# A graph layer on one core: which units of the last stage are scaled ahead and transposed, which are multiplied

## The chip, the core and the metric

The kernel runs on one core of a Trainium2 chip. A core has TensorE (PE in the profile, with its weight loads as PEld), VectorE (DVE), ScalarE (ACT), GpSimd (POOL) and SyncE (SP, which here only issues DMAs), a working memory of 128 partitions (SBUF), and PSUM, into which TensorE writes its results. The metric is the device time of one execution in microseconds; a time without an addition is the median of several runs.

## The reference

A graph layer over 12500 nodes with 256 features, a mixture of experts, a batch norm over the nodes, and a layer norm around all of it. What matters here is the end:

```python
def _forward(feats, ...):
    ...                                   # graph convolution m @ W_gc, residual, experts
    y = x + core                          # core: top-2 mixture of 64 experts
    mean = jnp.mean(y, axis=0)            # over the 12500 nodes, per feature
    var = jnp.mean((y - mean) ** 2, axis=0)
    return (y - mean) * jax.lax.rsqrt(var + BN_EPS) * gamma + beta

def _layernorm(x, axis=-1, eps=1e-05):    # over the 256 features, per node
    m = jnp.mean(x, axis=axis, keepdims=True)
    v = jnp.var(x, axis=axis, keepdims=True)
    return (x - m) / jnp.sqrt(v + eps)

out = _layernorm(x + _forward(x, ...))
```

## The kernel before

The nodes lie in 98 tiles of 128 (the last has 84). The program runs the edges and the first half of the experts, then the second half of the experts, then the last stage, which begins at line 2804 and is the only one that the change touches.

Through the whole last stage `y` lies in `acc`, seen as `acc2`: features on the partitions, in two halves `h` of 128, nodes along the free dimension. The loop at line 2825 adds the last contributions (line 2839), turns them (lines 2850 and 2851), takes the batch statistics (line 2857) and copies the sums back into `acc2` (line 2859). Lines 2880 to 2904 then make from the statistics, on VectorE, the scale `amp` and the shift `base` of each feature, and two diagonal matrices, `d_amp` and `d_base`.

From line 2905 on the nodes go through in 14 units. `order` (line 2861) numbers them: unit 0 is tiles 0 to 7, units 1 and 2 are the single tiles 96 and 97, units 3 to 13 are the other tiles in eights. `sets` (line 2862) groups them: [0], [1, 2], [3, 4], [5, 6], [7, 8], [9, 10], [11, 12], [13]. The input rows of unit u are in `xt[u]`, called `z`, [128 nodes x 8 tiles x 256], loaded by `fetch` (line 2865): the first ten ahead, unit u + 10 once unit u is handed out.

TensorE brings two tiles at a time back to nodes on the partitions, into a PSUM tile `q`, of which the pool `ps2` has five. There are two forms:

- **Scaled ahead and transposed** (`by_act`, before: odd units). First `acc2` of the unit is scaled and shifted in place, one instruction per half of 1024 columns: on GpSimd for units 1, 3 and 5 (line 2927), on ScalarE for units 7, 9, 11 and 13 (line 2932). Then TensorE transposes each half of each tile (line 2949).
- **Product** (before: even units). TensorE multiplies ones by `d_base` (line 2941) and adds each half times `d_amp` (line 2951); nothing is done ahead.

VectorE adds `q` to `z` and takes the row statistics, in one of two ways:

- **Squared** (before: units 0, 4, 6, 8, 10): one instruction per tile (line 2954) adds and also writes the row sum into a column of `m`; ScalarE then takes the sum of squares per tile (line 2968).
- **Otherwise**: an addition for two tiles (line 2961) and `bn_stats` for each (line 2963); a chain of eight small operations makes `m` and `ve` of them (lines 2975 to 2982), on GpSimd, in the last two sets on VectorE (`V_`).

At the end of a set: square root on ScalarE (line 2986), five small operations (lines 2987 to 2992, on VectorE but for the first), then each tile is normalised in place with one instruction: on GpSimd (line 3003) for units of eight with an even number, on ScalarE (line 3008) for the others; unit 13 is divided among three engines. The unit is handed out by a DMA of 1 MB on SP (line 3016); units 11, 12 and 13 go in two halves.

The small tiles of a set (`st`, `m`, `gap`, `ve`, `less`, `rs`, `rsq`, lines 2906 to 2912) come from the pool `two` with two buffers each, so a set's first write into `m` has to wait until an earlier set has given its buffer back, and the last reader of `m` is the normalisation.

The order of the instructions on each engine is chosen by a planner before the run, by the order of the program and by its own estimate of when operands are ready; each engine then runs its queue strictly in that order. Inside `tc.manual_schedule(engines=...)` the engines named keep the program's order.

Of the kernel before, what the change touches and what calls it, by code (L numbers as in the profile page):

```python
# [8 lines left out]
F32 = mybir.dt.float32  # L9
# [4 lines left out]
AF = mybir.ActivationFunctionType  # L14
ALU = mybir.AluOpType
# [4 lines left out]
P = 128  # L20
N = 12500
D = 256
# [3 lines left out]
EPS = 1e-5  # L26
# [140 lines left out]
def gnn_moe_kernel(  # L167
# [37 lines left out]
    def rows(t):  # L205
        return P if t < NT - 1 else RAG
# [191 lines left out]
    a = 0  # L398
# [10 lines left out]
    a = 0  # L409
# [2394 lines left out]
    with ExitStack() as stack:  # L2804
# [100 lines left out]
        for g, units in enumerate(sets):  # L2905
# [3 lines left out]
            m, gap, ve, less, rs, q_ = (  # L2909
# [4 lines left out]
            V_ = GP if g < len(sets) - 2 else V  # L2914
            at = 0
            for u in units:
                t0, n = order[u]
                r = rows(t0)
                z = xt[u][:r, :n]

                by_act = u % 2

                squared = not by_act and n == 8 and u != 12
                for h in range(2 * by_act):
                    y = acc2[:, h, t0 * P : (t0 + n - 1) * P + r]
                    if u in (1, 3, 5):
                        GP.tensor_scalar(
                            y, y, amp[:, h : h + 1], base[:, h : h + 1],
                            op0=ALU.mult, op1=ALU.add,
                        )  # L2930
                        continue
                    S.activation(
                        y, y, AF.Identity, bias=base[:, h : h + 1], scale=amp[:, h : h + 1]
                    )
                for i in range(0, n, 2):
                    k = min(2, n - i)
                    q = ps2.tile([P, 4, P], F32, name="q")
                    for j in range(k):
                        t = t0 + i + j
                        if not by_act:  # L2940
                            T.matmul(
                                q[:r, 2 * j : 2 * j + 2].rearrange("p a b -> p (a b)"),
                                ones_f[:, :r], d_base.rearrange("p a b -> p (a b)"),
                                start=True, stop=False,
                            )
                        for h in range(2):
                            to, y = q[:r, 2 * j + h], acc2[:, h, t * P : t * P + r]
                            if by_act:
                                T.transpose(to, y, ident)
                            else:  # L2950
                                T.matmul(to, y, d_amp[:, h], start=False, stop=h == 1)
                    if squared:
                        for j in range(k):
                            V.scalar_tensor_tensor(
                                z[:, i + j], q[:, 2 * j : 2 * j + 2].rearrange("p a b -> p (a b)"),
                                1.0, z[:, i + j], op0=ALU.mult, op1=ALU.add,
                                accum_out=m[:, at + i + j : at + i + j + 1],
                            )
                        continue
                    zi = z[:, i : i + k].rearrange("p t d -> p (t d)")  # L2960
                    V.tensor_add(zi, q[:r, : 2 * k].rearrange("p a b -> p (a b)"), zi)
                    for j in range(k):
                        V.bn_stats(st[:r, at + i + j], z[:, i + j])
                of = slice(at, at + n)
                if squared:
                    V.tensor_scalar_mul(m[:, of], m[:, of], -1.0 / D)
                    for i in range(n):
                        S.activation(
                            two.tile([P, D], F32, name="junk"), z[:, i], AF.Square,
                            bias=m[:, at + i : at + i + 1],  # L2970
                            accum_out=ve[:, at + i : at + i + 1],
                        )
                    V_.tensor_scalar(ve[:, of], ve[:, of], 1.0 / D, EPS, op0=ALU.mult, op1=ALU.add)
                else:
                    V_.tensor_sub(gap[:, of], st[:, of, 1], st[:, of, 4])
                    V_.tensor_mul(gap[:, of], gap[:, of], gap[:, of])
                    V_.tensor_scalar(gap[:, of], gap[:, of], 0.25, EPS, op0=ALU.mult, op1=ALU.add)
                    V_.tensor_add(ve[:, of], st[:, of, 2], st[:, of, 5])
                    V_.tensor_scalar(ve[:, of], ve[:, of], 1.0 / D, None, op0=ALU.mult)
                    V_.tensor_add(ve[:, of], ve[:, of], gap[:, of])  # L2980
                    V_.tensor_add(m[:, of], st[:, of, 1], st[:, of, 4])
                    V_.tensor_scalar(m[:, of], m[:, of], -0.5, None, op0=ALU.mult)
                at += n
# [10 lines left out]
            for u in units:  # L2994
# [3 lines left out]
                for i in range(n):  # L2998
                    by = GP if u % 2 == 0 and n == 8 else S
# [17 lines left out]
                fetch(u + 10)  # L3017

# [40 lines left out]
```

## Time and profile before

| | us |
|---|---|
| median of 3 runs | 2768.57 |
| lowest and highest run | 2766.28, 2773.52 |
| the profiled execution | 2766.83 |
| its span, first to last instruction | 2765.0 |
| of it: edges and first half of the experts, about | 2196 |
| second half of the experts, about | 443 |
| last stage, from its first loads on, about | 126 |

Over the whole span TensorE is busy 2389.1 us, GpSimd 1991.3, VectorE 1736.7 and ScalarE 687.6. These sums say little about the last 126 us, in which the change lies. How to read what follows: a timeline row has the start, the duration from the first start to the last end, the engine, the line, the operation with output and inputs, how many instructions it merges, and in brackets the engine's idle time before it and who ended it. A window row has for one stretch the busy time of each engine with its count of instructions, TensorE's granted clock as a share of the full one, the mean share of time that the 16 DMA engines were busy, and GB/s.

### The profile page before, as it was taken

How to read it: one execution, taken by the hardware profiler on the slowest of the kernel's cores; microseconds unless marked ns; L12 is line 12 of the kernel's file. 1: busy time of each engine (PE TensorE's matmuls, PEld its weight loads, DVE VectorE, ACT ScalarE, POOL GpSimd, SP SyncE). 2: the span in 40 equal slices, each digit the busy share in tenths (PEclk: the TensorE clock that was granted, in tenths of full speed). 3: DMA queues.
4: the chain of work that ended last, by engine and by line, in shares of the span. 5: the costliest groups of instructions: out<-in, count | busy, mean ns of one | idle time of the engine just before them, and what ended most of it. 6: DMA issues, size and time to landing. Idle time of an engine off the chain costs nothing.

```text
span 2765.0 us, 44989 instructions
## 1 busy us (share of the span) xinstructions
PE 2389.1 (86%) x13077; PEld 1830.1 (66%) x13077; DVE 1736.7 (63%) x7803; ACT 687.6 (25%) x2124; POOL 1991.3 (72%) x2240
## 2 busy tenths in 40 slices
PE   3967777777888887777999999999999899999986
PEld 3745555554666654545777777877768588988865
DVE  8979998754778864554655444454445645555558
ACT  1824344431111101101111111111111222222236
POOL 8777777777777777777777777777777666767615
PEclk9978999998999999997999999999999999999998
DMA  6963333336655555555677767877778778999888
GB/s 216 332 197 104 106 106 111 106 111 220 199 156 158 161 157 163 157 148 170 186 233 210 216 207 230 250 233 238 240 243 262 228 243 248 289 296 309 282 282 268
DMA packets 328938, 571.85 MB, mean 207 GB/s; under 512 B 79126, under 2 KB 229286, under 8 KB 328678
## 3 DMA queue, kind: packets, MB, share of 16 engines
q1 hardware_dynamic: 218424, 291.06, 33.1%
q0 software_dynamic: 96432, 263.13, 32.1%
q10 hardware_dynamic: 13822, 14.65, 1.7%
q8 instruction: 107, 1.75, 0.3%
q14 instruction: 153, 1.25, 0.1%
HBM read 494.61 MB, written 73.97 MB: 206 GB/s over the span
## 4 chain that ended last, share of the span: by engine, by line
PE 43%; POOL 19%; DMA 14%; issue 12%; DVE 7%; ACT 0%; SPq 0%; POOLq 0%; DVEq 0%; ACTq 0%
POOL ring L984 18%; DMA ring<-h_d,src_col 12%; PE p L1001 9%; PE yp L2357 8%; PE hp L2330 6%; PE bank L1225 3%; PE bank L1788 2%; PE yp_a L1788 2%; PE yp_a L1754 2%; PE bank L1754 2%; PE bank L1230 1%; POOL acc L1677 1%; PE yp_a L1162 1%; DVE acc L268 1%; PE xtp L2312 1%
## 5 line engine op out<-in xcount | busy, mean ns | idle before, releaser
L984 POOL DMA_INDIRECT ring<-h_d,src_col x1489 | 1416.6, 951 | 467.5 <-issue 402.0
L1001 PE MATMUL p<-ring,o 128*128 128x257 f32 (+1 forms) x3042 | 958.4, 419 | 246.6 <-DMA ring<-h_d,src_col 220.9
L1001 PEld LDWEIGHTS p<-ring,o 128*128 128x128 f32 x3042 | 526.7, 199 | 441.9 <-DMA ring<-h_d,src_col 311.3
L973 DVE TENSOR_SCALAR_CACHE_REDUCE o<-lane,rel 128x128 f32<-128x128 f32 x1489 | 450.4, 337 | 107.9 <-PE p L1001 107.1
L2357 PE MATMUL yp<-w,h 128*128 128x256 f32 (+4 forms) x968 | 225.1, 379 | 0.0
L1970 ACT ACTIVATE acc<-lane_b,acc 125x128 bf16<-125x128 bf16 x544 | 167.5, 389 | 177.9 <-DVE acc L1092 75.1
L2330 PE MATMUL hp<-xT,w 128*128 128x112 f32 (+17 forms) x1040 | 193.2, 332 | 1.8 <-DVE xT L2314 1.8
L2357 PEld LDWEIGHTS yp<-w,h 128*128 128x128 f32 (+4 forms) x968 | 169.5, 180 | 30.9 <-issue 0.9
L268 DVE TENSOR_TENSOR acc<-tab,acc 125x2450 bf16<-125x2450 bf16 (+1 forms) x136 | 184.4, 1356 | 3.9 <-PE bank L1979 3.2
L2330 PEld LDWEIGHTS hp<-xT,w 128*128 128x128 f32 x1040 | 163.2, 193 | 18.9 <-issue 2.9
L2335 ACT ACTIVATE h<-hp,b 128x112 f32<-128x112 f32 (+15 forms) x260 | 94.8, 417 | 321.7 <-issue 174.2
L1765 ACT ACTIVATE acc<-yp_a,acc 128x112 f32<-128x112 f32 (+19 forms) x150 | 57.8, 432 | 403.5 <-PE yp_a L1754 356.4
L1788 PE MATMUL bank<-acc 128*128 128x256 f32 (+7 forms) x672 | 156.1, 383 | 0.0
L1788 PEld LDWEIGHTS bank<-acc 128*128 128x128 f32 (+7 forms) x672 | 117.9, 178 | 28.5 <-issue 4.0
L2290 POOL DMA_INDIRECT xg<-xb_d,tables x101 | 97.4, 964 | 50.2 <-PE yp L2357 10.7
L1677 POOL DMA_INDIRECT acc<-xa_d,tables x110 | 104.2, 947 | 33.5 <-issue 31.4
L1754 PE MATMUL yp_a<-acc 128*128 128x112 f32 (+20 forms) x600 | 122.9, 346 | 1.7 <-DMA acc<-in_wpack 1.6
L1225 PE MATMUL bank<-wcat,acc 128*128 128x320 f32 x388 | 123.2, 442 | 0.0
L2384 POOL DMA_INDIRECT z_d<-yo,tables x81 | 81.5, 1006 | 55.5 <-DVE yo L2383 34.4
L1975 PEld LDWEIGHTS <-acc 125*128 125x128 bf16 x1156 | 83.1, 100 | 57.2 <-DVE acc L1092 15.8
L973 DVE DVE_READ_ACCUMULATOR o<-lane,rel 128x1 f32 x1489 | 119.4, 80 | 0.0
L1765 ACT ACTIVATE acc<-bank,acc 128x144 f32<-128x144 f32 (+18 forms) x106 | 44.8, 455 | 294.5 <-PE bank L1754 250.1
(452 smaller groups left out, 3943.2 us busy)
## 6 DMA issues: line engine op xcount, KB each, us to landing
acc<-in_wpack SPq DMA_DIRECT2D x128, 512.0 KB
w<-in_wpack SPq DMA_DIRECT2D x128, 512.0 KB
ring<-h_d,src_col POOLq DMA_INDIRECT x1489
tables<-h_d SPq DMA_DIRECT2D x99, 128.0 KB
z<-in_x SPq DMA_DIRECT2D x12, 1024.0 KB
acc<-in_x SPq DMA_DIRECT2D x13, 896.0 KB
h_d<-acc SPq DMA_DIRECT2D x13, 896.0 KB
zt<-z_d SPq DMA_DIRECT2D x22, 512.0 KB
```

The lines of the kernel that those rows point to most:

```text
L268: V.tensor_tensor(o.rearrange("p k (a b) -> p k a b", b=2), lane_b[:p, None, :n] .rearrange("p k (a b) -> p k a b", b=2) .to_broadcast([p, ...
L973: o_last[u] = V.tensor_scalar(o_of[u][:, j], lane, rel[:, c : c + 1], None, op0=ALU.is_equal, op1=ALU.add, accum_out=o_sum[:, c % 16 : c % ...
L984: i = GP.indirect_dma_start(out=h_row[:, :D], out_offset=None, in_=x if c < NE else h_d, in_offset=bass.IndirectOffsetOnAxis(ap=src_col[:, ...
L1001: i = T.matmul(p_of[g][:, :n], o_of[v][:, m], h_row[:, :n], start=j == 0, stop=last)
L1225: chain["dense"] = T.matmul(g[:r], acc2[:, k, a : a + r], wcat[:, k], start=k == 0, stop=k == 1 and not early,)
L1677: GP.indirect_dma_start(out=g, out_offset=None, in_=xa_d, in_offset=bass.IndirectOffsetOnAxis(ap=dense_a[:, c : c + 1], axis=0),)
L1754: T.matmul(hp, w1[:, c, j * P : (j + 1) * P], xT[:, c, :m], start=c == 0, stop=c == 1,)
L1765: S.activation(h1[:, j, :m], hp_of.pop((q, j)), AF.Gelu, bias=b1_a[i % 2][:, j : j + 1])
L1788: T.matmul(y, h1[:, j, k * P : k * P + n], w2[:, j], start=j == 0, stop=j == 3)
L1970: S.activation(s_los[k % 3][:, j], lane_b[:EP], AF.Sign, bias=nbs[u % 2][:, i, j : j + 1])
L2330: T.matmul(v, w1[:, c, j * P : (j + 1) * P], xT[:, c, :m], start=c == 0, stop=c == 1,)
L2357: T.matmul(yp[:r], h1[:, j, a : a + r], w2[:, j], start=j == 0, stop=j == 3,)
```

## The change

Five edits, all in the loop over units:

1. The form of the units. Scaled ahead and transposed are now units 0, 1, 3, 4, 6, 8, 10, 12 (before 1, 3, 5, 7, 9, 11, 13); product are 2, 5, 7, 9, 11, 13.
2. Unit 0 goes in pieces of 1, 1, 2, 2 and 2 tiles. Each piece is scaled by itself, the first on VectorE, the others on ScalarE. For the others GpSimd scales 1, 3, 4, 6 and ScalarE 8, 10, 12.
3. Squared are now units 3, 5, 7, 9, 11, so the first unit of each pair instead of the second.
4. GpSimd normalises units 3, 5, 7, 9, 12 (before 0, 4, 6, 8, 10, 12), ScalarE the others; unit 13 as before.
5. TensorE keeps the program's order in the whole loop.

The body of the loop moves into functions (`opened`, `unit`, `moved`, `pairs`) with the same operations.

```diff
-        for g, units in enumerate(sets):
+        def opened(g):
...
+        BY_ACT = (0, 1, 3, 4, 6, 8, 10, 12)
+
+        def pairs(n):
+            return [(i, min(2, n - i)) for i in range(0, n, 2)]
+
+        def unit(u, at, own, V_):
...
-                by_act = u % 2
-
-                squared = not by_act and n == 8 and u != 12
-                for h in range(2 * by_act):
-                    y = acc2[:, h, t0 * P : (t0 + n - 1) * P + r]
-                    if u in (1, 3, 5):
-                        GP.tensor_scalar(
+            by_act = u in BY_ACT
+
+            squared = u in (3, 5, 7, 9, 11)
+
+            def moved(a, b, by):
+                for h in range(2):
+                    y = acc2[:, h, a:b]
+                    if by is not S:
+                        by.tensor_scalar(
                             y, y, amp[:, h : h + 1], base[:, h : h + 1],
                             op0=ALU.mult, op1=ALU.add,
                         )
...
+            begins = [(0, 1), (1, 1), (2, 2), (4, 2), (6, 2)]
+            if u == 0:
+                for i, k in begins:
+                    moved((t0 + i) * P, (t0 + i + k) * P, V if i == 0 else S)
+            elif by_act:
+                moved(t0 * P, (t0 + n - 1) * P + r, GP if u in (1, 3, 4, 6) else S)
+            for i, k in begins if u == 0 else pairs(n):
+                q = ps2.tile([P, 4, P], F32, name="q")
...
+        phase = tc.manual_schedule(engines={mybir.EngineType.PE})
+        phase.__enter__()
+        for g, units in enumerate(sets):
+            V_ = GP if g < len(sets) - 2 else V
+            own = opened(g)
+            st, m, gap, ve, less, rs, q_ = own
+            at = 0
+            for u in units:
+                unit(u, at, own, V_)
+                at += order[u][1]
...
-                    by = GP if u % 2 == 0 and n == 8 else S
+                    by = GP if u in (3, 5, 7, 9, 12) else S
...
+        phase.__exit__(None, None, None)
```

More of the change, by code (lines that the diff above doesn't have):

```diff
@@ L2908, in gnn_moe_kernel @@
                 V.memset(st, 0.0)
-            m, gap, ve, less, rs, q_ = (
+            return st, *(
                 two.tile([P, 16], F32, name=name)
@@ L2912, in gnn_moe_kernel @@
             )
[L2914 to L2919, printed above, removed]
-                by_act = u % 2
-                squared = not by_act and n == 8 and u != 12
-                for h in range(2 * by_act):
-                    y = acc2[:, h, t0 * P : (t0 + n - 1) * P + r]
-                    if u in (1, 3, 5):
-                        GP.tensor_scalar(
+        BY_ACT = (0, 1, 3, 4, 6, 8, 10, 12)
[3 more added lines that the diff above has]
+            st, m, gap, ve, less, rs, q_ = own
+            t0, n = order[u]
+            r = rows(t0)
+            z = xt[u][:r, :n]
+            by_act = u in BY_ACT
[5 more added lines that the diff above has]
+                        by.tensor_scalar(
                             y, y, amp[:, h : h + 1], base[:, h : h + 1],
@@ L2934, in gnn_moe_kernel @@
                     )
-                for i in range(0, n, 2):
-                    k = min(2, n - i)
-                    q = ps2.tile([P, 4, P], F32, name="q")
-                    for j in range(k):
[L2939 to L2971, printed above, removed]
-                        )
[L2973 to L2982, printed above, removed]
@@ new lines, in unit @@
+            of = slice(at, at + n)
+            if squared:
+                V.tensor_scalar_mul(m[:, of], m[:, of], -1.0 / D)
+                for i in range(n):
+                    S.activation(
+                        two.tile([P, D], F32, name="junk"), z[:, i], AF.Square,
+                        bias=m[:, at + i : at + i + 1],
+                        accum_out=ve[:, at + i : at + i + 1],
+                    )
+                V_.tensor_scalar(ve[:, of], ve[:, of], 1.0 / D, EPS, op0=ALU.mult, op1=ALU.add)
+            else:
+                V_.tensor_sub(gap[:, of], st[:, of, 1], st[:, of, 4])
+                V_.tensor_mul(gap[:, of], gap[:, of], gap[:, of])
+                V_.tensor_scalar(gap[:, of], gap[:, of], 0.25, EPS, op0=ALU.mult, op1=ALU.add)
+                V_.tensor_add(ve[:, of], st[:, of, 2], st[:, of, 5])
+                V_.tensor_scalar(ve[:, of], ve[:, of], 1.0 / D, None, op0=ALU.mult)
+                V_.tensor_add(ve[:, of], ve[:, of], gap[:, of])
+                V_.tensor_add(m[:, of], st[:, of, 1], st[:, of, 4])
+                V_.tensor_scalar(m[:, of], m[:, of], -0.5, None, op0=ALU.mult)
```

26 lines of the change are left out of this document (25 added, 1 removed).

## The prediction

> **What bounds the kernel now.** All edits lie behind the making of `d_base`, so I read first the table of windows over the last stage, to see which engine has no room.
>
> ```profile
> 2685.00:2700.00 15.00, 15.00 (x105) 13.80 (x104) 9.71 (x39) 13.14 (x26) 8.90 (x25) 1.00 1.09 345
> 2700.00:2715.00 15.00, 14.83 (x106) 13.48 (x106) 13.45 (x59) 8.03 (x25) 10.39 (x31) 1.00 0.65 201
> 2715.00:2730.00 15.00, 14.71 (x103) 13.54 (x102) 14.04 (x56) 12.24 (x39) 9.47 (x30) 1.00 1.02 341
> 2730.00:2745.00 15.00, 11.40 (x85) 10.40 (x83) 14.33 (x57) 12.10 (x37) 7.72 (x18) 1.00 0.70 232
> 2745.00:2765.00 20.00, 0.00 (x0) 0.00 (x0) 10.57 (x38) 7.43 (x17) 7.55 (x14) 0.50 0.84 277
> ```
>
> The columns of busy time are PE, PEld, DVE, ACT, POOL. TensorE is full at first and finished soon after 2740. VectorE has slack only in the first stretch (9.7 of 15 us); then it is nearly full and outlasts TensorE by 15 us. So TensorE is late at the start, VectorE carries the middle. The end is not VectorE's, as the output queue and the DMA columns show:
>
> ```profile
> 2746.99 12.09 SPq L3016 DMA_DIRECT2D out<-z  x8
> ```
> ```profile
> 2751.76 7.32 SPq L3016 DMA_DIRECT2D out<-z  x6
> ```
> ```profile
> 2745.00:2746.00 1.00, 0.00 (x0) 0.00 (x0) 1.00 (x5) 1.00 (x3) 1.00 (x3) 0.51 0.85 284
> 2747.00:2748.00 1.00, 0.00 (x0) 0.00 (x0) 1.00 (x5) 0.00 (x0) 0.00 (x0) 0.50 0.07 26
> ```
> ```profile
> 2735.00:2740.00 5.00, 5.00 (x38) 4.74 (x36) 5.00 (x18) 5.00 (x14) 3.74 (x7) 1.00 0.07 25
> 2755.00:2760.00 5.00, 0.00 (x0) 0.00 (x0) 1.17 (x3) 1.28 (x3) 1.03 (x2) 0.50 1.03 340
> 2760.00:2765.00 5.00, 0.00 (x0) 0.00 (x0) 0.00 (x0) 0.00 (x0) 0.00 (x0) 0.50 0.69 228
> ```
>
> Units 9 and 10 are handed out from 2746.99, and data moves from about 2748 (only 26 GB/s before). From there 5 MB (units 9 to 13, 5.24 million bytes) go at 340 GB/s without a gap: 15.4 us, to 2763.4 (228 GB/s x 5 us is 3.3 us of full rate); the span ends 1.6 us later. Yet from 2735 to 2740 the DMA stood nearly still: outputs came late and together.
>
> **Part 1: unit 0.**
>
> ```profile
> 2684.44 0.15 DVE L2898 TENSOR_TENSOR base<-bet,base 128x2 f32<-128x2 f32 x1
> 2684.71 0.48 DVE L2904 TENSOR_SCALAR d_base<-idents,base 128x128 f32<-128x128 f32 x2
> 2687.54 0.42 DVE L2954 SCALAR_TENSOR_TENSOR z<-q,z 128x256 f32<-128x256 f32 x1 [2.35 <-PE q L2951]
> 2693.51 0.42 DVE L2961 TENSOR_TENSOR z<-q,z 128x256 f32<-128x256 f32 x1
> ```
> ```profile
> 2681.19 4.56 PE idle L448 x10
> 2685.75 0.43 PE q L2941 x2
> 2686.18 0.44 PE q L2951 x4
> 2693.86 1.75 PE q L2949 x16
> ```
>
> In the chain of waits a product tile costs TensorE 0.43 + 0.44 = 0.87 us, a transposed one 1.75 / 8 = 0.22. Unit 0 today: VectorE idles 2.35 us, then runs at TensorE's pace until 2693.5. After the change two 128x128 scalings come on VectorE, priced like the two of `d_base`, 0.48 us. They end by 2685.7, whichever pair is first. TensorE is held by the matmuls of L448 until 2685.75 anyway; one transposed tile later VectorE starts, at about 2686.2. Its work on an unsquared unit is that of unit 5, from 2704.70 to about 2709.95:
>
> ```profile
> 2704.70 0.69 DVE L2961 TENSOR_TENSOR z<-q,z 128x512 f32<-128x512 f32 x1
> 2708.56 1.39 DVE L2963 BATCH_NORM_STATS2 st<-z 128x6 f32<-128x256 f32 x4
> ```
> ```profile
> 2684.63 9.16 ACT L2932 ACTIVATE acc<-acc,base,amp 128x1024 f32<-128x1024 f32 x8 [1.68 <-DVE base L2898]
> 2742.57 4.04 ACT L3008 ACTIVATE z<-z,m,rs 128x256 f32<-128x256 f32 x8 [1.91 <-DVE m L2992]
> ```
>
> 5.25 us plus 0.25 for the pair that is split makes 5.5, so unit 0 ends at 2691.7: **1.8 us earlier**. ScalarE keeps ahead: a 256-column instruction has a pitch of 4.04 / 8 = 0.505 us, two make a pair of tiles ready per 1.0 us against VectorE's 1.3.
>
> The same moment is a place where GpSimd could get in VectorE's way: it starts scaling unit 1 at 2684.80.
>
> ```profile
> 2684.80 5.77 POOL L2927 TENSOR_SCALAR acc<-acc,amp,base 128x128 f32<-128x128 f32 x6 [53.88 <-DVE base L2898]
> 2751.30 0.45 DVE L2976 TENSOR_TENSOR gap<-gap 128x8 f32<-128x8 f32 x1
> 2753.90 0.17 DVE L2989 TENSOR_TENSOR rsq<-rs 128x8 f32<-128x8 f32 x1
> ```
>
> Beside GpSimd's normalisation a small VectorE operation took 0.45 us, without it 0.17. But the two of `d_base`, across GpSimd's start, took 0.48 together, as much as without a neighbour; I take nothing, with 0.5 as the other end. The Trainium skill, "SBUF — State Buffer", section "Who interferes with whom", says that a VectorE `tensor_scalar` in a two-port mode and a GpSimd instruction lock each other out whole, and whoever issues first goes first. By that rule the scalings would wait only if GpSimd were ahead, for an instruction of about half a microsecond: unit 0 would gain 1.3 instead of 1.8.
>
> **Part 2: which units are squared.** The rows of the table of lines, and the first L2954 of unit 4:
>
> ```profile
> L2963 DVE BATCH_NORM_STATS2 st<-z 128x6 f32<-128x256 f32 x57 | 21.0, 407 | 0.0
> L2961 DVE TENSOR_TENSOR z<-q,z 128x512 f32<-128x512 f32 x28 | 18.3, 676 | 0.0
> L2954 DVE SCALAR_TENSOR_TENSOR z<-q,z 128x256 f32<-128x256 f32 x40 | 14.9, 412 | 6.7 <-PE q L2951 5.5 <-ACT z L3008 1.2
> L2968 ACT ACTIVATE junk<-z,m 128x256 f32<-128x256 f32 x40 | 19.7, 494 | 4.4 <-POOL gap L2976 3.8 <-DVE m L2966 0.6
> ```
> ```profile
> 2701.94 0.42 DVE L2954 SCALAR_TENSOR_TENSOR z<-q,z 128x256 f32<-128x256 f32 x1 [1.16 <-ACT z L3008]
> ```
>
> The counts stay: 40 tiles squared, 58 not. But unit 0 becomes dear, where VectorE waited anyway (counted above), and unit 11 cheap, where it did not: 5.25 less 8 x 0.345 is **2.5 us**. (0.345 is the pitch of L2954: eight of them from 2701.94 to 2704.70.) Unit 11's chain of eight operations, on VectorE in that set, goes too; two remain: about **0.8 us**.
>
> **Part 3: TensorE.** Eight tiles fewer as products save 8 x 0.65 = 5.2 us, all on unit 0, already counted. Afterwards a pair takes TensorE 7.0 + 1.75 = 8.8 us, and VectorE 2.8 + 5.25 and some 0.85 of small operations, 8.9; VectorE stays the bound, by little. The fixed order is nearly the one seen today; nothing for it.
>
> **Part 4: ScalarE, GpSimd, the queues.** ScalarE scales for unit 0 about 4 us and 6 x 1.145 = 6.9 us, where it had 9.2; the 40 squares and the normalisations keep their number. GpSimd scales two halves of 1024 columns more, about 1.2 us each (six of L2927, two of them short, took 5.77), and normalises 8 tiles less. Both have room. No DMA is added; unit 0 leaves earlier, and behind it on SP's queue the load of unit 10, with time to spare.
>
> **Part 5: a wait that is added.** Just ahead of the row of 2701.94 stands on ScalarE:
>
> ```profile
> 2700.82 1.09 ACT L3008 ACTIVATE z<-z,m,rs 128x256 f32<-128x256 f32 x2 [2.11 <-DVE m L2992]
> ```
>
> Today unit 4's first L2954 waits 1.16 us for the normalisation of units 1 and 2: it writes `m` of the third set and needs one of two buffers. After the change unit 3, eight tiles sooner, writes `m` first. VectorE reaches it at 2691.7 + 1.4 (units 1 and 2) = 2693.1. When is a buffer free?
>
> ```profile
> 2719.09 0.21 POOL L2975 TENSOR_TENSOR gap<-st 128x8 f32<-128x8 f32 x1 [2.35 <-DVE st L2963]
> 2720.56 0.20 POOL L2980 TENSOR_TENSOR ve<-ve,gap 128x8 f32<-128x8 f32 x1
> 2723.35 4.34 POOL L3003 TENSOR_SCALAR z<-z,rs,m 128x256 f32<-128x256 f32 x8 [1.96 <-DVE m L2992]
> ```
>
> Unit 0's statistics end at 2691.7; GpSimd's eight operations take 1.7, root and hand-over 0.4, the five on VectorE, at 0.17 and a little between them, 1.1 when it is free, ScalarE's eight 4.04, and up to half a microsecond for what is running: about 2699.3. The wait is **6.2 us** if VectorE does nothing else, and behind it stand all its additions. It can do something: TensorE puts unit 3 into four of the five buffers `q`, and unit 4, which needs no `m` for its additions, can go through the fifth, a pair per 1.4 us, until 2698.6. Then 0.7 us are left, and unit 5's products, which found no buffer, come late by about 1.6: **2.3 us**. The planner decides. Today it puts additions of unit 5 ahead of unit 4's scaling of `m` (2704.70 above), so it does fill; I take 2.3, with 0 and 6.2 as ends. The 1.16 us of today go.
>
> For later sets the buffer is free some 8.7 us after the statistics end (just ahead of 2719.09, to 2727.69, in the rows above) and wanted after 8.9. ScalarE's squares of the next unit come just then; I take 0.5 us for that.
>
> **Part 6: the end, and the sum.** VectorE arrives at unit 12 earlier by 1.8 + 2.5 + 0.8 + 1.2 - 2.3 - 0.5 = 3.5 us. Units 9 and 10 no longer end on squares, and are out before 2742; the queue at the end then starts with the halves of units 11 and 12. Their first today is at 2751.76; 1.0 to the first data, 3 MB in 9.2 us and 1.6 make 2763.6, that is 1.4 less than 2765.0 without any shift. So the span shrinks by 3.5 + 1.4 = 4.9 us, to 2760.1. The profiled execution lies 1.8 us above its span (2766.83), so it would take 2761.9; against the median of the runs, 2768.57, the same 4.9 give **2763.7 us**, 0.18% faster. A measurement of this kernel tells about 0.3% (8.3 us) from no change.
>
> **The rivals.**
>
> - *The wait for `m` isn't filled.* 6.2 instead of 2.3: gain 1.0, 2767.6. For it: one VectorE queue in a fixed order, which today stands still 1.16 us for the same buffer. Against it: the filling named above. TensorE, with all five buffers full, would stand still for six microseconds, and its clock could fall:
>
> ```profile
> 2741.00:2742.00 1.00, 0.40 (x4) 0.16 (x2) 1.00 (x6) 0.00 (x0) 0.00 (x0) 1.00 1.03 342
> ```
>
>   Its last matmul ends at 2741.4, and at 2745 to 2746 the granted clock is 0.51 (above): some 3.6 us of standing still halve it. If it takes as long to come back, unit 5's products run 3.6 us at half speed and lose 1.8: 2769.4. The Trainium skill, "TensorE: Matmul & The Clock Gate", section "HAM oscillation — how this bites in real kernels", states the same rule, no gaps over about 3.4 us; the trace agrees, with 3.6. By that rule this rival, not the forecast, pays.
> - *Outputs stay as late as they are.* If units 9 and 10 still come out after 2746, because ScalarE does the squares of unit 11 first, the end stays where it is: gain 0, 2768.6. For it: ScalarE is busy 12 of 15 us. Against: that set no longer waits for squares at its end.
> - *Slower.* The buffers of `m` decide every set. Today a set is normalised 14 us after VectorE leaves it (2713.6, the end of the row below, to 2727.69). Above 8.9 us each further microsecond costs half a microsecond per set. With 14 for four sets that is 4 x 2.6 = 10.4 us, with the opening unfilled: 4.9 - 3.9 - 10.4 = 9.4 us slower, 2778.0. Against it: the 14 us come from squares at the end of the set, which move to its start.
>
> ```profile
> 2713.24 0.41 DVE L2954 SCALAR_TENSOR_TENSOR z<-q,z 128x256 f32<-128x256 f32 x1
> ```
>
> - *Clearly faster.* No wait for `m` (2.3 and 0.5 saved) and VectorE's three waits for the root (together 1.8 us, one of them the row below) gone: gain 4.9 + 2.8 + 1.8 = 9.5, 2759.1.
>
> ```profile
> 2721.33 0.25 DVE L2988 RECIPROCAL rs<-rs 128x16 f32<-128x16 f32 x1 [0.96 <-ACT rs L2986]
> ```
>
> - That the edit does nothing at all is excluded for unit 0: its products were what VectorE waited for.
>
> **How the numbers follow.** Forecast 0.42, wait not filled 0.22, outputs late 0.13, slower 0.06, clearly faster 0.17. Faster by over 0.3% is the last case: 0.17; slower the fourth: 0.06; the rest, 0.77, is within 0.3%. The range reaches from the clearly faster case, 2758.5, to the unfilled wait with the clock's price, 2769.5; beyond lie the slower case and the edges of the others.
>
> **What would show it.** VectorE's first addition near 2686.2, unit 0 finished near 2691.7; the idle time ahead of unit 3's first L2954 against 2.3; additions of unit 4 ahead of it; the output of units 9 and 10 before 2742; the end set by the halves of units 11 and 12; granted clock 1.00 until the last matmul. A different order by the planner on ScalarE would make it wrong most easily.

## The result and the profile after

The changed kernel took **2784.17 us** (median of 6 runs), the kernel before 2766.39 (median of 6): a ratio of 1.006, with a 95% interval of 1.0048 to 1.0071. The change makes the kernel slower by 0.6%; forecast were 2763.7 us and a range from 2758.5 to 2769.5. The profiled execution of the changed kernel took 2783.34 us, its span is 2781.5, which is 16.5 more than before.

The first reading splits these 16.5 us at the making of `base`, the last step ahead of the edits, which stood at 2684.44 before. From the timeline of the changed kernel:

```profile
2696.71 0.15 DVE L2898 TENSOR_TENSOR base<-bet,base 128x2 f32<-128x2 f32 x1
```

**12.3 us were lost before the first edited instruction**, and 4.2 behind it: from `base` to the end of the span it was 80.56 us before (2765.0 - 2684.44) and is 84.79 now. I call this time the *stage* from here on.

**Ahead of the edit.** The costliest group of instructions on the page, in the kernel before:

```profile
L984 POOL DMA_INDIRECT ring<-h_d,src_col x1489 | 1416.6, 951 | 467.5 <-issue 402.0
```

and in the changed one:

```profile
L984 POOL DMA_INDIRECT ring<-h_d,src_col x1489 | 1429.0, 960 | 463.5 <-issue 403.7
```

These are GpSimd's gathers of the edge stage, busy time and mean first. All 1489 together take 12.4 us more. It is no single slow one; the view of that line (shortest, median, longest in ns), before:

```profile
L984 POOL DMA_INDIRECT ring<-h_d,src_col x1489: 940/947/3075, 153.5 to 2174.7; - x187
```

and after:

```profile
L984 POOL DMA_INDIRECT ring<-h_d,src_col x1489: 947/953/4215, 153.5 to 2183.9; - x187
```

The shortest and the median both grew by 6 to 7 ns. Nothing in these instructions was changed: both traces list the same GpSimd operations, on the same tiles and in the same order, up to the last stage.

Longer gathers matter here because GpSimd has hardly any slack between them. The only other large group on GpSimd in that stretch are the gathers of L1677, before:

```profile
L1677 POOL DMA_INDIRECT acc<-xa_d,tables x110 | 104.2, 947 | 33.5 <-issue 31.4
```

and after:

```profile
L1677 POOL DMA_INDIRECT acc<-xa_d,tables x110 | 104.9, 953 | 33.5 <-issue 31.1
```

("issue" is idle time in which the engine waited for nothing that the profile shows.) Gathers and issue time of both lines add up to 1954.2 us before, of the 2021.2 from the first start to the last start in the view above. GpSimd waited for other engines for some 67 us only. In the changed kernel it is 1968.7 of 2030.4. So 14.5 us more of gathers with their issue and 5.3 less of waiting make the last gather 9.2 us later. The other 3.1 of the 12.3 us came between it and `base`.

**In the last stage.** VectorE sets the end again: its last operation ends 8.8 us before the span does, in both kernels. So its time from `base` to there is what counts. The table of windows over just that stretch (columns as in the prediction), before:

```profile
2684.44:2756.17 71.73, 56.49 (x396) 51.47 (x394) 62.67 (x247) 53.20 (x141) 44.23 (x115) 0.92 0.86 280
```

after:

```profile
2696.71:2772.74 76.03, 56.45 (x364) 48.55 (x362) 61.75 (x244) 58.72 (x155) 43.41 (x116) 0.88 0.83 270
```

VectorE does 0.9 us less work and needs 4.3 us more, so its idle time grew by 5.2. The view of the waits names whom it waited for (us in total, times, longest), before:

```profile
DVE z L2954 <- PE q L2951: 5.5, 5, 2.4
DVE rs L2988 <- ACT rs L2986: 2.1, 4, 1.0
DVE z L2954 <- ACT z L3008: 1.2, 1, 1.2
```

and after:

```profile
DVE rs L3010 <- ACT rs L3008: 5.9, 5, 2.4
DVE z L2966 <- POOL z L3025: 3.5, 2, 1.8
DVE z L2966 <- PE q L2963: 2.8, 3, 1.0
DVE z L2973 <- PE q L2961: 1.2, 4, 0.4
```

The wait for unit 0's products is gone, as forecast. In its place stand waits for roots (5.9), for `m` (3.5) and for the products of unit 5 (2.8).

The opening, from the timeline of the changed kernel:

```profile
2697.06 8.19 POOL L2933 TENSOR_SCALAR acc<-acc,amp,base 128x128 f32<-128x128 f32 x8 [53.41 <-DVE base L2898]
2698.44 0.76 DVE L2973 TENSOR_TENSOR z<-q,z 128x256 f32<-128x256 f32 x2 [0.42 <-PE q L2961]
2705.20 0.22 POOL L2987 TENSOR_TENSOR gap<-st 128x8 f32<-128x8 f32 x1
2706.92 0.21 ACT L3008 ACTIVATE rs<-ve 128x8 f32<-128x8 f32 x1 [1.66 <-POOL ve L2992]
2707.03 2.36 ACT L2938 ACTIVATE acc<-acc,base,amp 128x1024 f32<-128x1024 f32 x2
2707.16 0.20 DVE L3010 RECIPROCAL rs<-rs 128x8 f32<-128x8 f32 x1 [2.41 <-ACT rs L3008]
2708.51 1.11 PE L2961 MATMUL q<-idents,acc 128*128 128x128 f32 x4 [3.28 <-DVE z L2973]
2709.25 0.14 DVE L3014 TENSOR_TENSOR m<-m,rs 128x8 f32<-128x8 f32 x1
2710.21 0.20 ACT L3008 ACTIVATE rs<-ve 128x2 f32<-128x2 f32 x1 [0.82 <-POOL ve L2992]
2710.45 5.03 ACT L3030 ACTIVATE z<-z,m,rs 128x256 f32<-128x256 f32 x10
2714.86 0.41 DVE L2966 SCALAR_TENSOR_TENSOR z<-q,z 128x256 f32<-128x256 f32 x1
2719.48 0.42 DVE L2966 SCALAR_TENSOR_TENSOR z<-q,z 128x256 f32<-128x256 f32 x1 [0.85 <-PE q L2963]
```

VectorE starts early, as it should (second row), and is done with unit 0 at 2703.8. Then nothing follows quickly. GpSimd's queue has all eight of its scalings ahead of unit 0's chain of small operations, which begins at 2705.20. VectorE's queue has the reciprocal of unit 0's root ahead of everything that it could do, so it stands still for 2.41 us. ScalarE does the scalings of unit 12 next, which nobody needs yet; they end at 2709.39, just when unit 0's `m` is ready (the row of 2709.25), and so cost nothing. What holds unit 0's normalisation until 2710.45 is the root of units 1 and 2, which stands ahead of it and waits 0.82 us for GpSimd's chains. All buffers `q` are full meanwhile, TensorE stands still for 3.28 us, and the windows show what that does to its clock:

```profile
2704.00:2706.00 2.00, 1.09 (x8) 0.85 (x8) 0.75 (x3) 1.26 (x2) 2.00 (x7) 1.00 1.10 347
2708.00:2716.00 8.00, 5.13 (x18) 3.75 (x19) 7.08 (x27) 6.63 (x13) 3.05 (x18) 0.50 0.65 209
2718.00:2720.00 2.00, 2.00 (x16) 1.90 (x15) 1.15 (x8) 1.62 (x7) 0.00 (x0) 1.00 0.65 194
```

At 0.50 from 2708 to 2716 unit 4's transposes arrive a pair per 1.9 us, and unit 5's products begin late. Only their first pair runs at half speed. The waits for the other three (the row of 2719.48, 0.85 us, and two of 0.98) come after the clock's return: TensorE has no lead left, and a pair of products takes it 1.75 us, where VectorE adds a pair in 0.8.

In the middle, VectorE's waits for `m`, and the normalisation on GpSimd that ends just then:

```profile
2726.84 4.32 POOL L3025 TENSOR_SCALAR z<-z,rs,m 128x256 f32<-128x256 f32 x8 [3.80 <-DVE m L3014]
```
```profile
2731.19 0.42 DVE L2966 SCALAR_TENSOR_TENSOR z<-q,z 128x256 f32<-128x256 f32 x1 [1.76 <-POOL z L3025]
2751.03 0.42 DVE L2966 SCALAR_TENSOR_TENSOR z<-q,z 128x256 f32<-128x256 f32 x1 [1.77 <-POOL z L3025]
```

These are the first additions of units 7 and 11, each of which writes the buffer of `m` that units 3 and 7 still need. At the end, unit 13's root stands behind unit 11's normalisation on ScalarE:

```profile
2766.06 4.04 ACT L3030 ACTIVATE z<-z,m,rs 128x256 f32<-128x256 f32 x8 [2.24 <-DVE m L3014]
2770.00 0.19 ACT L3008 ACTIVATE rs<-ve 128x8 f32<-128x8 f32 x1
```
```profile
2770.23 0.20 DVE L3010 RECIPROCAL rs<-rs 128x8 f32<-128x8 f32 x1 [2.26 <-ACT rs L3008]
```

### The profile page after: what moved, and what is told of

The parts are those of the page before. It is cut to its first block, busy times and chain, and to the rows that moved or that the text cites. A ratio compares the mean times of both kernels' runs of the same rounds, so it can differ in the third digit from the quotient of the medians.

```text
span 2781.5 us, 44929 instructions
## 1 busy us (share of the span) xinstructions
PE 2401.7 (86%) x13045; PEld 1833.9 (66%) x13045; DVE 1735.1 (62%) x7799; ACT 692.6 (25%) x2138; POOL 2003.1 (72%) x2241
## 4 chain that ended last, share of the span: by engine, by line
PE 41%; POOL 21%; DMA 14%; issue 12%; DVE 6%; ACT 1%; SPq 0%; DVEq 0%; POOLq 0%; ACTq 0%
POOL ring L984 19%; DMA ring<-h_d,src_col 11%; PE p L1001 9%; PE yp L2357 7%; PE hp L2330 6%; PE bank L1788 3%; PE yp_a L1754 3%; PE bank L1225 3%; PE yp_a L1788 3%; PE bank L1754 2%; PE bank L1230 1%; POOL acc L1677 1%; PE xtp L2312 1%; PE tab L1427 1%; DVE acc L268 1%
## 5 line engine op out<-in xcount | busy, mean ns | idle before, releaser
L984 POOL DMA_INDIRECT ring<-h_d,src_col x1489 | 1429.0, 960 | 463.5 <-issue 403.7
L1001 PE MATMUL p<-ring,o 128*128 128x257 f32 (+1 forms) x3042 | 970.7, 423 | 250.8 <-DMA ring<-h_d,src_col 229.2
L1765 ACT ACTIVATE acc<-yp_a,acc 128x112 f32<-128x112 f32 (+19 forms) x150 | 57.6, 431 | 403.6 <-PE yp_a L1754 340.0
L1677 POOL DMA_INDIRECT acc<-xa_d,tables x110 | 104.9, 953 | 33.5 <-issue 31.1
```

What stands on the lines that cost most here:

```text
L984: i = GP.indirect_dma_start(out=h_row[:, :D], out_offset=None, in_=x if c < NE else h_d, in_offset=bass.IndirectOffsetOnAxis(ap=src_col[:, ...
L1001: i = T.matmul(p_of[g][:, :n], o_of[v][:, m], h_row[:, :n], start=j == 0, stop=last)
L1677: GP.indirect_dma_start(out=g, out_offset=None, in_=xa_d, in_offset=bass.IndirectOffsetOnAxis(ap=dense_a[:, c : c + 1], axis=0),)
L1765: S.activation(h1[:, j, :m], hp_of.pop((q, j)), AF.Gelu, bias=b1_a[i % 2][:, j : j + 1])
```

## The experiments

Two theories go in. **Upstream**: either the edit itself brings the slower gathers (A), or they vary from build to build (B). **Last stage (C)**: the waits just shown make the 4.2 us; the rival is the fixed order of TensorE.

### Controls, the order, the buffers

*e1*: the kernel before with 20 blank lines.

> The kernel before, unchanged but for blank lines, so that its line numbers move by 20. Of the 16.5 us by which the changed kernel's span was longer, 12.3 were there before the first edited instruction: GpSimd's gathers (L984, 1489 of them) had a median of 953 ns instead of 947 and a smallest of 947 instead of 940. Theory A, the step comes with the edit: here 940 and 947 ns, the scale `base` made at 2684 us, the time within 0.1% of the kernel before. Theory B, the step differs from build to build or from load to load of a program, whatever its last stage: here it may as well show 947 and 953 ns and a `base` at 2696, 0.45% slower.

Gathers 942/947 ns, `base` at 2684.71, stage 80.59; ratio 1.0004 (0.9994 to 1.0014). The step doesn't change between two builds of one program, which speaks against B in the form "from build to build".

*e2*: edit 5 alone.

```diff
+        phase = tc.manual_schedule(engines={mybir.EngineType.PE})
+        phase.__enter__()
         for g, units in enumerate(sets):
...
+        phase.__exit__(None, None, None)
```

> The kernel before, with TensorE's order in its last loop fixed (edit 5 alone). From `base` to the end of the span it took 80.6 us before and 84.8 after the change. Theory C, the added 4.2 us come from waits of VectorE (for `m`, for a root, for late products after TensorE's clock fell): here nothing of that, 80.6 within 0.5 us. Rival, the fixed order costs it: 82 or more. Upstream: theory A, which ties the slower gathers to the changed instruction stream of the last stage, gives 947 ns (2684 us), since this stream hardly changes; theory B gives either step.

Gathers 941/947, stage 80.50, the same waits as before; ratio 1.0001 (0.9992 to 1.0011). The fixed order costs the kernel before nothing.

*e3*: the changed kernel without these three lines.

> The changed kernel without the fixed order (edits 1 to 4). Theory C: the order hardly matters, from `base` to the end of the span 84.8 us within 0.7, with the waits of 1.8 us for `m` at units 5 and 9, and the clock at 0.50 for some 8 us after TensorE has stood still about 3.3 us. Rival, the fixed order costs it: 82 or less. Upstream: theory A 953 ns and `base` at 2696.7; theory B either step.

Gathers 947/953, `base` at 2697.80, stage 86.10; ratio 1.0066 (1.0047 to 1.0086). The rival falls: without the fixed order the stage isn't shorter. (The waits for `m` stand ahead of units 7 and 11, not of 5 and 9 as the expectations have it.)

*e4*: four buffers for the small tiles.

```diff
-                two.tile([P, 16], F32, name=name)
+                two.tile([P, 16], F32, name=name, bufs=4)
```

> The changed kernel with four buffers instead of two for the small tiles `m`, `gap`, `ve`, `less`, `rs` and `rsq` of a set, so that a set's first write into `m` no longer waits for a normalisation two sets back. Theory C: the two waits of 1.76 and 1.77 us at units 5 and 9 go, as does the idle time of TensorE that lowered the clock at the start (3.3 us of standing still, about 2.8 us of late products); from `base` to the end of the span 84.8 - 3.5 to 84.8 - 6.3, that is 78.5 to 81.3. Rival, the roots and ScalarE's and GpSimd's queues come late anyway and the same time is lost at them: 83.5 to 85. Upstream: theory A 953 ns; theory B either step.

Stage **78.70**, 6.1 less than the changed kernel's; ratio 1.0037 (1.0024 to 1.005). VectorE's windows row and waits:

```profile
2698.80:2768.60 69.80, 53.17 (x364) 47.98 (x362) 61.12 (x244) 58.42 (x155) 43.64 (x116) 0.91 0.90 294
```
```profile
DVE rs L3010 <- ACT rs L3008: 7.7, 7, 2.4
DVE z L2973 <- PE q L2961: 0.4, 1, 0.4
DVE z L2966 <- PE q L2963: 0.3, 1, 0.3
```

The waits for `m` are gone, and with them nearly all the waiting for TensorE (2.8 + 1.2 before, 0.7 now), although TensorE still stands still for 3.42 us here: unit 3 no longer has to let unit 4 pass, so its pairs lie ready in `q`. 1.8 us come back as waits for roots. One line thus turns the stage of the change from 4.2 us worse into 1.9 better than before. The kernel is slower all the same, because its gathers take 948/954 ns and `base` comes at 2698.80.

### What moves the gathers

A first candidate was the length of TensorE's program, the longest. All kernels with gathers of 953 or 954 ns so far had 106 packets in the row of the queue that brings instructions, all with 947 ns had 107. On the page of the kernel before and of the changed one (packets, MB, share):

```profile
q8 instruction: 107, 1.75, 0.3%
```
```profile
q8 instruction: 106, 1.74, 0.3%
```

*e5*: the changed kernel with small matmuls at the end of TensorE's queue, which nobody reads. *e6*: the kernel before with fewer of those that only keep TensorE warm.

```diff
+        for _ in range(24):
+            T.matmul(idle[:, :32], ones_b, ones_b[:, :32], start=True, stop=True)
```
```diff
-        warm(idle, 36)
+        warm(idle, 14)
```

> The changed kernel with 24 small matmuls (32 columns, nobody reads them) behind the last unit, at the end of TensorE's queue. The profile's row of the queue q8 (instructions) has 107 packets of 16.4 KB in all kernels with fast gathers and 106 in all with slow ones; TensorE's program is the longest, and the edit shortens it. Theory D: the length of TensorE's program, when it crosses a block of 16 KB, moves something in memory, and the gathers L984 take 953 instead of 947 ns for that reason. Here 107 packets again, gathers 940/947 ns, `base` about 2684 instead of 2697, span about 2769 (2781.5 - 12.3), and a time about 2771, still slower than before by the 4.2 us of the last stage. Rival, the step comes with another part of the edit (GpSimd's, VectorE's or ScalarE's program): 947/953 ns, a time near 2784.

> The other way round: the kernel before with 14 instead of 36 of the matmuls that only keep TensorE warm at the start of the last stage (they compute nothing that is read), so that its program is 44 instructions shorter. Theory D: 106 packets in q8, gathers 947/953 ns, `base` some 10 us or more later than 2684. Rival: 940/947 ns.

The theory falls: e5 has 107 packets and gathers of 947/953. (e6 kept its 107 packets, with 940/946, and so tested nothing; e7 below has 106 and 940/946.) This chip was another one: the kernel before takes 3272 us on it (more on that below), and there e5 is not slower than before, 1.0002 (0.9981 to 1.0023). Stages: e5 85.57, e6 80.46. e6 ran only once, as e9 to e12 below did, and so has no ratio.

*e7*: e4 with unit 0's chain on VectorE. *e8*: e7 with the matmuls of e5.

```diff
-            V_ = GP if g < len(sets) - 2 else V
+            V_ = GP if 0 < g < len(sets) - 2 else V
```

> The kernel of e4_after_four with the chain of eight small operations of unit 0 on VectorE instead of GpSimd, where it stood behind eight scalings of 8.2 us. In e4 VectorE then waited 2.44 us for the root of unit 0 and TensorE stood still for 3.42 us. Theory C: these waits go for some 1.6 us of small operations on VectorE; from `base` to the end of the span 76.5 to 78.2 (78.7 in e4). Rival, the end is set by the outputs alone: 78.7 within 0.4. Upstream by theory D: 953 ns.

> The kernel of e7_four_chain with the 24 matmuls of e5_after_pad at the end. Theory D and theory C together: gathers 940/947 ns, `base` at 2684 to 2685, a stage of 76.5 to 78.5, a span of 2761 to 2763 and a time of about 2764, 0.1 to 0.2% faster than before. Rival to D: near 2777, like e7.

Stages 79.62 and 80.17, both longer than e4's: a miss. The waits for roots fell from 7.7 to 4.8 us, but VectorE has 1.7 us more to do and unit 5's products came late by 2.4 again. On this chip neither differs from the kernel before: 1.0005 (0.999 to 1.0019) and 1.0007 (0.9987 to 1.0027). The gathers: 940/946 in e7, **943/949** in e8, which differs from e7 in 24 matmuls at the very end. There are more than two levels, and TensorE's program can move them.

*e9 to e12*: memsets of one column on GpSimd at the end of the program, six and two in the changed kernel, two and three in the kernel before.

```diff
+        spare = one.tile([P, 1], F32, name="spare")
+        for _ in range(6):
+            GP.memset(spare, 0.0)
```

> The changed kernel with six one-column memsets of a spare tile on GpSimd at the end of the program, so that GpSimd's program is as long as before the change (the edit took six instructions from it). So far the gathers L984 had a median of 946 or 947 ns (before and its variants, e7), 949 (e8) and 953 or 954 (after, e3, e4, e5). Theory E: the length of GpSimd's own program decides. Here 940/947 ns and `base` some 12 us earlier than in the changed kernel. Rival F, the step follows from the layout of the whole program in memory and no single length: 953 or 949 or 947, without a rule.

> The changed kernel with two such memsets on GpSimd. The lengths with fast gathers so far (5434 and 5422 instructions) and those with slow ones (5428, 5431) differ in their remainder by four: 2 for the fast, 0 and 3 for the slow. With two more it is 5430, remainder 2. Theory E with that rule: 947 ns. Theory E without it (the distance from 5434): 953. Rival F: either.

> The kernel before with two such memsets at the end, of which the built program is one GpSimd instruction longer (5435, remainder 3). Theory E with the rule of four: 953 ns. Rival F: either; the kernel before has shown 947 in four builds.

> The kernel before with three such memsets, two GpSimd instructions longer (5436, remainder 0). Theory E with the rule of four: 953 ns. Rival F: either.

Medians 953, 953, **949**, 946. GpSimd's length isn't the rule either: e9's is as before the change, and its gathers are long. (On this chip, too, the kernel before takes longer, 3271 us; the stages are 86.34, 85.21, 80.58 and 80.28.) But the first row of e11 (a kernel with nothing of the change) has a step of its own:

```profile
L984 POOL DMA_INDIRECT ring<-h_d,src_col x1489: 943/949/3659, 204.8 to 2613.5; - x187
```

*e13, e14*: five and thirteen such memsets on VectorE, in the changed kernel and in e4. *e15*: the kernel before with one more set's chain on GpSimd.

```diff
-            V_ = GP if g < len(sets) - 2 else V
+            V_ = GP if g < len(sets) - 1 else V
```

> The changed kernel with five one-column memsets of a spare tile on VectorE at the end of the program, which make VectorE's program about as long as before. Of twelve programs those with gathers of 946 to 949 ns have 9234 VectorE instructions or more, those with 953 or 954 ns 9233 or fewer; GpSimd's length (e9 to e12) and TensorE's (e5, e6) do not decide. Theory G: VectorE's length decides. Here 946 to 949 ns, `base` at 2684 to 2688 where the kernel before has 2684, and a time near 2772, slower than before only by the 4.2 us of the last stage. Rival F, the layout of the whole program: anything from 946 to 954.

> The kernel of e4_after_four (gathers 954 ns, a stage of 78.7 us) with 13 such memsets on VectorE at the end, as long on VectorE as before. Theory G: 946 to 949 ns; with the stage of e4 the span is some 1.9 us shorter than that of the kernel before, a time near 2766, ratio 0.999. Rival F: 954 ns and 1.0037, as e4, or anything between.

> The kernel before with the small operations of the next to last set (units 11 and 12) on GpSimd instead of VectorE, which takes 17 instructions from VectorE's program (9221). Theory G: gathers 953 ns in a kernel that has nothing of the change, `base` at 2696, a time near 2780. Rival F: 946 to 954. From `base` to the end of the span 80.6 within 1.

953, **957** and 949: VectorE's length falls too. The ratios: e13 1.006 (1.0042 to 1.0077), e14 1.0029 (1.0014 to 1.0044), e15 1.0007 (0.9997 to 1.0018). e14's stage is 78.67, as e4's; e15's is 82.48 and not 80.6, because roots behind GpSimd's chains cost VectorE 7.8 us of waiting instead of 2.1.

What these runs do give is a series. Nine programs were profiled on chips where the kernel before takes 2766 to 2772 us:

| program | gather, median ns | all 1489, us | `base` at, us |
|---|---|---|---|
| before | 947 | 1416.6 | 2684.44 |
| e2 | 947 | 1418.5 | 2689.30 |
| e1 | 947 | 1419.8 | 2684.71 |
| e15 | 949 | 1422.1 | 2688.02 |
| e13 | 953 | 1428.8 | 2699.02 |
| changed | 953 | 1429.0 | 2696.71 |
| e3 | 953 | 1429.2 | 2697.80 |
| e4 | 954 | 1432.3 | 2698.80 |
| e14 | 957 | 1433.7 | 2701.43 |

`base` moves with the sum of the gathers, about one for one, with a scatter of some 3 us: the four with 947 to 949 ns have 1419.3 us of gathers and `base` at 2686.6 on average, the five with 953 to 957 ns 1430.6 and 2698.8. From the start of the last gather to `base` it takes 509.6 to 512.8 us in all nine, without a relation to the step (512.6 in e1 and e2, 509.6 in e4), so the 3.1 us that the changed kernel lost there are of the size of this scatter. That says what most of the 12.3 us are. It doesn't say why a program has one step and not another, and in this series it is the kernels with the changed stage that have the long gathers.

*e16*: e7 once more, to see on such a chip whether a program with all edits and fast gathers starts its last stage early. *e17*, *e18*: e7 and e4 with half of unit 11's normalisation on VectorE.

```diff
+                    if u == 11 and i >= 4:
+                        by = V
```

> The kernel of e7_four_chain once more (all edits of the change, four buffers, unit 0's chain on VectorE), which there had gathers of 946 ns. Where the kernel before takes about 2768 us: if the duration of the gathers sets where the last stage begins, `base` here comes at 2683 to 2687, as in the kernel before, although the last stage is that of the change; with a stage of 79.6 the span is 2763 to 2767 and the ratio 0.998 to 1.001. If the later `base` belongs to the edits themselves and the gathers only go with it, `base` comes at 2695 or later and the ratio is 1.004. The gathers again 946 ns, if a program keeps its step from chip to chip.

> The same with four of the eight normalisations of unit 11 on VectorE instead of ScalarE, where unit 13's root stood behind them (VectorE waited 2.3 us for it, then the last 3 MB went out). Theory C: the end follows VectorE's last operation by 8.8 us; the wait falls to about 0.5 for 1.5 us more of work, so a stage of 78.5 to 79.2 instead of 79.6. Rival, the 3 MB at the end decide and start earlier: 77.5. Gathers: by theory F any step.

> The same split of unit 11 in the kernel of e4_after_four (stage 78.7): 77.5 to 78.3. Gathers: any step from 946 to 957 ns.

e16 again fell on a chip where the kernel before takes 3278 us, so its question stays open (1.0002 there, 0.9983 to 1.0021; e17 0.9996, 0.9978 to 1.0014). The one program that was profiled on two chips kept its step: e7 had 940/946 ns on one, and e16 on another:

```profile
L984 POOL DMA_INDIRECT ring<-h_d,src_col x1489: 940/946/3599, 209.5 to 2616.5; - x187
```

On these chips the step decides nothing: `base` comes at 3191.60 in e16 with 946 ns and at 3191.37 in e18 with 953. The group of lines in e18 shows why:

```profile
L984 POOL DMA_INDIRECT ring<-h_d,src_col x1489 | 1428.2, 959 | 854.0 <-issue 394.9 <-remote 178.8 <-PE p L1001 119.8
```

GpSimd idles 854 us between its gathers there instead of 462 to 468, and only 394.9 of it are issue, so they don't set the pace.

The end: stages 79.44 (e17) and **78.43** (e18), 0.2 to 0.3 better than without the split; expected was more. In e17 the longest wait for a root fell from 2.3 to 1.2 us, but the four normalisations cost VectorE more than thought beside GpSimd's, 0.56 each (e18):

```profile
3254.56 2.25 DVE L3027 TENSOR_SCALAR z<-z,rs,m 128x256 f32<-128x256 f32 x4
```

The rival, that the outputs alone set the end, falls: in all twenty profiles, e17 and e18 too, the span ends 8.8 to 8.9 us after VectorE's last operation. e18 is the best last stage found, 2.1 us shorter than before, and on its chip 0.28% faster than the kernel before: 0.9972 (0.995 to 0.9994). That is some 9 us, of which the stage explains 2.1; where the rest comes from was not shown, and on these chips `base` scatters by 14 us from program to program (3181.08 in e7 to 3195.54 in e6). Where the kernel before takes 2768 us e18 wasn't run; with gathers of 953 ns the series above puts its `base` some 12 us later than before, so it would lose about 10 us there (an estimate).

## Why the prediction was wrong

**What bounds the kernel.** "All edits lie behind the making of `d_base`, so I read first the table of windows over the last stage": this is the step that failed most. It took for granted that what stands ahead of an edit stays as it is. 12.3 of the 16.5 us lie there. The runs show that the same gathers take 946 to 957 ns in different programs, and that the one program profiled on two chips kept its value. Theory A falls in its plain form: a program with all the edits can have 946 (e7, e16), and the kernel before goes to 949 with two memsets at its end (e11). The length of one engine's program alone doesn't set it: e7 and e8 differ in TensorE's only, the kernel before and e11 in GpSimd's only, and each pair differs in its step. That it follows from how the whole program lies in memory is an argument, not shown. That longer gathers make `base` late, and don't only go with it, follows from GpSimd's row: it is at gathers or issuing them for 1954.2 of 2021.2 us. The series of nine bears it out; a run that has all edits and short gathers where the kernel before takes 2768 us is missing (e16 was to be it). No row of the profile before shows that the gathers' duration would change.

**Part 1 was right.** VectorE's first addition came 1.73 us behind `base` (forecast 2686.2, so 1.8), and unit 0 was done 2.0 us earlier than before (forecast 1.8). GpSimd hardly got in the way: VectorE's two scalings, begun when GpSimd was already scaling, took 0.65 us together instead of 0.48.

**Parts 2 and 3 were right.** VectorE's work fell by 0.9 us; the terms (unit 0 dearer by 2.7, unit 11 cheaper by 2.5 and 0.8) make 0.6. TensorE's order cost nothing (e2, e3).

**Part 4, "Both have room", was wrong in its question.** ScalarE and GpSimd have room on average. What counted was the place in their queues: eight scalings ahead of unit 0's chain, the root of units 1 and 2 ahead of unit 0's normalisation. The first buffer of `m` came free 2.9 us later than worked out: eight of the ten normalisations from 2710.45 on end at 2714.5, 17.8 us behind `base` and not 14.9. GpSimd's scalings cost 1.4 of it and the root of units 1 and 2 1.1; the five operations on VectorE, with statistics and an addition between them, took 2.2 instead of 1.1.

**Part 5 had the mechanism right and its sizes too small.** Unit 4's additions went ahead of unit 3 through the fifth buffer, as written. But the opening cost VectorE 2.41 us of waiting for a root, which the sum doesn't have, and 2.8 us for unit 5's products, where 2.3 stood for everything; TensorE stood still for 3.28 us, and its clock fell. For the later sets "the buffer is free some 8.7 us after the statistics end" failed: unit 3's squares and five small operations, put between additions of 0.4 to 0.7 us each, held it until 2731.16, 13.5 us after VectorE left that set at 2717.7. The filling itself had moved unit 3's squares to the end of the set, because unit 4 passed unit 3. In the set of units 7 and 8 it was 10.9 us: unit 7's squares stood behind unit 6's normalisation on ScalarE until 2739.51. 0.5 us was forecast, 3.5 measured. e4 shows the price of it all: with four buffers the stage is 6.1 us shorter.

**Part 6.** The 1.4 us from the output queue didn't come. The end kept its 8.8 us behind VectorE, so the reading that the end is the output queue's and not VectorE's was wrong. Units 9 and 10 were handed out at 2759.80, 63.1 us behind `base`, no earlier than before (62.6); 57.6 was forecast. And the waits for roots, left at today's 2.1 us, became 5.9.

**The rivals.** "Slower, the buffers of `m` decide every set" (2778.0, a chance of 0.06) names the right mechanism, but they decided every second set, 3.5 us and not 10.4. The clock, held for a rival's price only, fell although the wait *was* filled. What remained of the prediction: from `base` on it said 4.9 us less and it was 4.2 more.

## What to carry to other kernels

When an edit lets a later unit write a small per-set tile sooner, give that tile another buffer first: here four buffers instead of two were worth 6 us, where the edit without them lost 4. Before an engine is said to have room, read what its queue holds ahead of the instruction that the next stage waits for. And compare two builds at the last step ahead of the edit before anything else: a few nanoseconds on an instruction that runs 1489 times can outweigh the edit, and no reading of the edit finds them.

## What the hardware showed unexpectedly

**One instruction, several durations.** The gathers above: medians from 946 to 957 ns, for the same operation on the same tiles. The gathers of L1677 moved with them, from a mean of 947 to 953.

**The clock falls at fixed times, not after a fixed pause.** The changed kernel's last matmuls before the pause, and the windows that hold the fall and the return:

```profile
2704.14 1.09 PE L2961 MATMUL q<-idents,acc 128*128 128x128 f32 x8 [0.42 <-DVE z L2973]
```

```profile
2706.80:2707.20 0.40, 0.00 (x0) 0.00 (x0) 0.04 (x1) 0.28 (x2) 0.31 (x3) 0.72 1.10 348
2717.00:2717.50 0.50, 0.50 (x5) 0.50 (x4) 0.50 (x3) 0.00 (x0) 0.00 (x0) 0.78 1.04 346
```

TensorE's pause began at 2705.23. A mean of 0.72 puts the fall at 2706.98, 1.7 us into it; 0.78 puts the return at 2717.22. In e4:

```profile
2706.23 1.09 PE L2961 MATMUL q<-idents,acc 128*128 128x128 f32 x8 [0.42 <-DVE z L2973]
2710.75 0.63 PE L2961 MATMUL q<-idents,acc 128*128 128x128 f32 x4 [3.42 <-DVE rs L3013]
```

```profile
2711.50:2712.00 0.50, 0.40 (x3) 0.43 (x4) 0.50 (x3) 0.50 (x3) 0.41 (x3) 0.72 1.09 344
2715.00:2715.50 0.50, 0.50 (x4) 0.45 (x4) 0.09 (x1) 0.50 (x3) 0.00 (x0) 0.86 0.08 27
```

There the pause began at 2707.32 and the clock fell at 2711.72, 4.4 us later, when TensorE had already gone back to work; it came back at 2715.14. The lengths at half speed are 10.24 and 3.42 us, three times 3.41 and once. In each of the two traces all changes of the granted clock, 83 and 79 of them, lie on one grid of 3.413 us. The windows of that grid around the fall, first in the changed kernel, then in e4:

```profile
2703.57:2706.98 3.41, 1.25 (x10) 0.85 (x8) 1.18 (x4) 1.75 (x3) 3.16 (x11) 1.00 1.10 349
2706.98:2710.39 3.41, 1.11 (x4) 0.71 (x4) 2.88 (x10) 2.59 (x4) 3.00 (x18) 0.50 1.11 349
```

```profile
2704.90:2708.31 3.41, 2.00 (x17) 1.53 (x15) 1.94 (x7) 2.45 (x3) 3.41 (x9) 1.00 1.10 350
2708.31:2711.72 3.41, 0.75 (x5) 0.57 (x6) 2.44 (x15) 2.68 (x4) 3.00 (x18) 1.00 1.10 347
```

TensorE was busy for 1.25 us of 3.41 in the window that ended with the fall in the changed kernel. In e4 the window in which the pause began still had 2.00 us and changed nothing; the next had 0.75, and the clock fell at its end. In the traces of all twenty kernels full speed ended only behind windows with at most 63% busy, and half speed only behind windows with at least 78% (by the profile's modelled ends of matmuls). The Trainium skill, "TensorE: Matmul & The Clock Gate", section "Part 1: The HAM clock gate (the "warmup" mystery)", describes this as a free-running window of 4096 cycles, about 3.4 us; the trace agrees, and it explains why my 3.6 us from one place of the profile could not be carried to another. It also fits that the six kernels with the stage of the change and two buffers, all with a pause of some 3.3 us at the same place, lost full speed 1.4 (e9) to 4.6 us (e3) after its beginning, for three or four times 3.41 us, and had stages from 84.8 to 86.4 us.

The grid isn't what made e4 better. Where the fall came at nearly the same place behind `base` (12.2 us in e5 and 12.0 in e14, 13.1 in e3 and 12.9 in e4), the kernels with two buffers stayed at half speed for 10.24 us and those with four for 3.41, and the stages are 85.57 against 78.67 and 86.10 against 78.70.

**Chips differ ahead of the last stage.** On some, the kernel before took 3271 to 3278 us instead of 2766 to 2772, and GpSimd idled 850 to 864 us between gathers instead of 462 to 468. The last gather began at 2616.5 in e6, where it began at 2174.7 before, and from there to `base` it took 579.0 us instead of 509.7; the last stage took 80.5 us on both kinds (e1, e6). Why was not tried.
